# Two PSUM results of a graph-attention layer leave PSUM through ScalarE and are taken up later by VectorE

## The chip, the cores and the metric

The kernel runs on one core of a Trainium2 chip. The metric is the device time of one execution in microseconds (us), as the median of several runs. Five engines work side by side, each through its own instructions in order: TensorE (PE; its weight loads are listed apart as PEld), VectorE (DVE), ScalarE (ACT), GpSimd (POOL) and SyncE (SP, which issues most of the transfers). They wait for each other by semaphores.

## The reference

`x` has 6250 nodes of 768 features; 100000 directed edges come sorted by destination (`dst`), with random sources (`src`). To these edges each node adds a loop to itself.

```python
def gat_conv(h, W, a_src, a_dst, heads):          # one attention layer
    h = (h @ W).reshape(n, heads, -1)
    alpha_s = (h * a_src[None]).sum(-1)
    alpha_d = (h * a_dst[None]).sum(-1)
    e = leaky_relu(alpha_s[src] + alpha_d[dst], 0.2)
    e = exp(e - segment_max(e, dst)[dst])
    alpha = e / segment_sum(e, dst)[dst]
    return segment_sum(h[src] * alpha[:, :, None], dst)

h = maximum(layernorm(x), 0)
h = relu(gat_conv(h, W1, ..., heads=4) + b1)      # layer 1: 4 heads of 64
h = relu(gat_conv(h, W2, ..., heads=1) + b2)      # layer 2: 1 head of 256
out = x + relu(h @ Wm1 + bm1) @ Wm2 + bm2         # 256 -> 256 -> 768
```

## The kernel before

**Stages.** The profile's span has four of them: features of all nodes (layer norm, `h @ W1`; up to about 200 us), the edges of layer 1 (about 205 to 1350 us), a border (to about 1450), and the edges of layer 2 with the closing MLP. Nodes lie in 49 tiles of 128 (`NT`). Edges lie in tiles of 128, four tiles to a group (`TPG`), 196 groups (`NG`), four groups to a "tile step" `t` (`t, j = divmod(g, 4)`). One loop runs over the groups `g`; the order of each engine's instructions is the order in which this loop writes them out (a manual schedule), and the waits follow from who reads and writes which buffer.

**A group.** GpSimd gathers the table rows of the sources by indirect transfers, eight groups ahead (`gather(g + 8)`, L645, one transfer per edge tile). Rows of two edge tiles are a pair, and each group has two. For a pair (`pair`, L712, L722, L724) VectorE forms the weight of each edge per head from the row's own factors and the destination's factors and scales the row by it into `hw` (10 buffers). TensorE multiplies `hw` with a 0/1 matrix `hot` (5 buffers, written by VectorE at L673 for the next group), which adds up the rows by destination in `o_ps` (L736, three PSUM banks, one for two groups). Every second group VectorE adds such a product to the running sum (L753) and ScalarE copies its finished quarters (`sum`, L762). When a node tile is complete, its node step runs in pieces over the following half groups (`Node1.steps`): VectorE adds the tile's own loop (`mine` from L939, sum at L945), divides (L956, L958), TensorE turns the result (L915), ScalarE adds the bias and clips (`rT`, L921), TensorE multiplies by `W2` (L966), ScalarE writes the next table's row tile (`kept`, L969 and the lines after it), and SP stores it.

**Destination factors.** The factors of the destinations reach the edges by a product too. VectorE builds a 0/1 mask for eight edge tiles (`make_mask`, L662, from rows fetched at L610; SP also stores it for layer 2), and TensorE multiplies each edge tile's mask with the window of node factors (`meet`, L691, 16 tiny matmuls a tile step). The products come in three parts per head, which VectorE adds up in place in PSUM (`join`, L699); `pair` works in that same PSUM tile `e_ps`, of which there are two. In the loop, `meet(t + 1)` is written at j = 0 and `join(t + 1)` at the end of j = 3.

**Completing rows.** 46 edge tiles of layer 1 (23 pairs, list `SOON`) are gathered early, during the first stage, when the last m node tiles are not yet computed (m from 2 to 20). Those rows are held in DRAM, brought back in time (`soon_back`), and what they lack is added by products with the feature tiles that stayed in SBUF. For pair number i and half t (k = 2i + t) VectorE compares the sources with the m missing tiles' node numbers (`soon_hits`, L379, into `soon_hit`, 128 x up to 2560, one buffer in a pool with `bufs=1`), TensorE makes the m products (`soon_missing`, L389, into a PSUM bank of tag "n", two banks shared with the node steps), and VectorE adds them to the row (`soon_whole`, L396):

```python
row = G[soon_pair[i]][:, t]
nc.vector.scalar_tensor_tensor(row, row, soon_ok[:, i, t:t + 1], soon_p.pop(k),
                               ALU.mult, ALU.add)
```

One pair is due every eight groups. For pair i the groups are: even half, hits in 8i + 1, products in 8i + 3, taken up in 8i + 5; odd half, hits in 8i + 5, products in 8i + 6, taken up in 8i + 8. The pair itself is used in group 8i + 11. Within a group the hook stands between the two pairs, the taking up ahead of the next hits.

PSUM's eight banks in this stage: three of `o_ps`, two of tag "n", two of tag "e" (`e_ps`), one of constants.

Of the kernel before, what the change touches and what calls it, by code (L numbers as in the profile page):

```python
# [10 lines left out]
F32 = mybir.dt.float32  # L11
BF16 = mybir.dt.bfloat16
I32 = mybir.dt.int32
AF = mybir.ActivationFunctionType
ALU = mybir.AluOpType
# [55 lines left out]
def kernel(  # L71
# [99 lines left out]
        nc.sync.dma_start(wt, WT.rearrange("(j p) f -> p j f", p=P))  # L171
        return wt, a

    def scores_in(ps, w, wt, a, K, H):
        nc.vector.tensor_copy(w[:, :, HID:], scores(ps, wt, a, K, H))

    def scores(ps, wt, a, K, H):
        p = ps.tile([P, K, 2 * H], F32, name="aps", tag="e")
        for k in range(K):
            for j in range(KH):  # L180
                nc.tensor.matmul(p[:, k], wt[:, j, k * P:(k + 1) * P], a[:, j],
                                 start=(j == 0), stop=(j == KH - 1))
        return p
# [151 lines left out]
    soon_i = const.tile([P, len(SOON), 2], I32, name="soon_i")  # L335
    soon_ok = const.tile([P, len(SOON), 2], F32, name="soon_ok")
    soon_d = dram.tile([len(SOON), P, 2 * TW[1]], F32, name="soon_d")
    soon_G, soon_of, soon_p, soon_hit = {}, {}, {}, {}
    soon_pair = {i: pair for pair, i in SOON_AT.items()}

    def soon_places(i):
# [42 lines left out]
    def soon_missing(k):  # L384
        if 0 <= k < 2 * len(SOON):
            there, hit = SOON[k // 2], soon_hit.pop(k)
            soon_p[k] = ps.tile([P, TW[1]], F32, name="missing1", tag="n")
            for T in range(there, NT):
                nc.tensor.matmul(soon_p[k], hit[:, T - there], kept[T], start=(T == there),  # L389
                                 stop=(T == NT - 1))  # L390

    def soon_whole(G, k):
        if 0 <= k < 2 * len(SOON):
            i, t = divmod(k, 2)
            row = G[soon_pair[i]][:, t]
            nc.vector.scalar_tensor_tensor(row, row, soon_ok[:, i, t:t + 1], soon_p.pop(k),  # L396
                                           ALU.mult, ALU.add)

    mask_d = dram.tile([NU * P, 8 * P], BF16, name="mask_d")
# [219 lines left out]
    def layer_edges(layer, H, node, pre, matched, pre_pool):  # L619
# [4 lines left out]
        with tc.tile_pool(name=f"eg{layer}", bufs=5) as eg, \  # L624
                tc.tile_pool(name=f"hw{layer}", bufs=10 if layer == 1 else 14) as hwp, \
                tc.tile_pool(name=f"sum{layer}", bufs=4) as sums, \
                tc.tile_pool(name=f"sm{layer}", bufs=4) as sm:
            G, hot, e_ps, o_ps = {}, {}, {}, {}

            def tiles(g):  # L630

# [51 lines left out]
            def meet(t):  # L683

                if t >= NT:
                    return
                e_ps[t] = ps.tile([P, 16, 6 * H], F32, name="e_ps", tag="e")
                for u, at, a, b in ranges(t):
                    m = mask.pop(u)
                    for k in range(a, b):  # L690
                        nc.tensor.matmul(e_ps[t][:, at + k, :3 * H], m[:, k * P:(k + 1) * P],  # L691
                                         pre.win[:, 2 * u + 2], start=True, stop=True)

            def join(t):
                if t >= NT:
                    return
                (_, _, a, _), (_, at, _, b) = ranges(t)
                T = slice(a, at + b)
                nc.vector.tensor_reduce(  # L699
                    e_ps[t][:, T, 3 * H:4 * H],  # L700
                    e_ps[t][:, T, :3 * H].rearrange("p t (h k) -> p t h k", k=3), AX.X, ALU.add)

            def pair(g, p):

                if 2 * p not in tiles(g):
                    return
                Gp = G.pop(TPG // 2 * g + p)
                e1, e2 = ((Gp[:, :, RW[1]:RW[1] + 4], Gp[:, :, RW[1] + 4:]) if layer == 1 else
                          (Gp[:, :, HID:HID + 1], Gp[:, :, HID + 2:]))
                at = TPG * (g % 4) + 2 * p  # L710
                rho, v, w = (e_ps[g // 4][:, at:at + 2, k * H:(k + 1) * H] for k in range(3, 6))
                nc.vector.tensor_mul(v, e2, rho)  # L712
                if layer == 2:
                    w = sm.tile([P, 2, H], F32, name="w")
                    nc.vector.tensor_max(w, v, e1)  # L715
                    hw = hwp.tile([P, 2, P], F32, name="hw")
                    for t in range(2):
                        k = TPG * g + 2 * p + t
                        nc.vector.tensor_scalar(hw[:, t], iota_ps, dcol[:, k:k + 1], w[:, t],  # L719
                                                ALU.is_equal, ALU.mult)  # L720
                else:
                    nc.vector.tensor_max(w, v, e1)  # L722
                    hw = hwp.tile([P, 2, H, C + 1], F32, name="hw")
                    nc.vector.tensor_mul(  # L724
                        hw, Gp[:, :, :RW[1]].rearrange("p t (h c) -> p t h c", h=H),
                        w.unsqueeze(3).to_broadcast([P, 2, H, C + 1]))
                u = g // 2
                if u not in o_ps:
                    o_ps[u] = ps.tile([P, RW[layer]], F32, name="o_ps", tag="o", bufs=3)
                for t in range(2):  # L730
                    k = 2 * p + t
                    if layer == 2:
                        l, r = hw[:, t], Gp[:, t]
                    else:
                        l, r = hot[g][:, k], hw[:, t].rearrange("p h c -> p (h c)")
                    nc.tensor.matmul(o_ps[u], l, r[:, :RW[layer]], start=(g % 2 == 0 and k == 0),  # L736
                                     stop=(g % 2 == 1 and k == tiles(g)[-1]))
# [74 lines left out]
            if layer == 2:  # L812
                first_whole(pre_pool, layer)
            meet(0)
            join(0)
            def taken_up(h):

# [27 lines left out]
            for g in range(NG):  # L845
                t, j = divmod(g, 4)
                if layer == 2 and g >= NG - 2:
                    if g == NG - 2:
                        last_pairs()
                    continue  # L850
                if g == NG - 2:
                    at_end.append(g)
                gather(g + AHEAD)
                pair(g, 0)
                if g == NG - 1:
                    pair(g, 1)
                if g == NG - 2:
                    gather_up(NU - 2)
                advance(g)
                if taken_up(2 * g) is not None:  # L860
                    gather_up(taken_up(2 * g))
                if g <= NG - 4:
                    make_hot(g + 1)
                if g in (NG - 4, NG - 3):
                    make_hot(g + 2)
                if j == 0:
                    if layer == 1:
                        fetch_rows(t + 4)
                    node.prefetch(t)
                    meet(t + 1)  # L870
                elif j == (2 if t < NT - 1 else 1):
                    node.ahead(t)
                elif j % 2:
                    make_mask((g + 7) // 2)
                if layer == 1:
                    for i, at in enumerate(SOON_GROUP):
                        for k, hits_at in ((2 * i, at - 10), (2 * i + 1, at - 6)):
                            if g == hits_at + 3 + (k % 2 == 0):
                                soon_whole(G, k)
                            if g == hits_at:  # L880
                                soon_hits(pre_pool, k)
                            if g == hits_at + 1 + (k % 2 == 0):
                                soon_missing(k)
                        if g == at - 13:
                            soon_sources(pre_pool, i)
                if g == NG - 3:
                    idle_ps.append(ps.tile([P, 4 * P], F32, name="idle_ps", tag="e"))
                if g >= NG - 3:
                    stay_warm(3)
                if g < NG - 1:  # L890
                    pair(g, 1)
                advance(g, 1)
                if j == 3:
                    join(t + 1)
                if taken_up(2 * g + 1) is not None:
                    gather_up(taken_up(2 * g + 1))
                if NG - 3 <= g < NG - 1:
                    stay_warm(3)
                hot.pop(g, None)
                if layer == 1 and g == NG - 6:  # L900
                    first_sources(2)
# [23 lines left out]
    with tc.tile_pool(name="w2p", bufs=1) as wp, tc.tile_pool(name="wk2", bufs=2) as wk:  # L925
# [4 lines left out]
        class Node1:  # L930
# [4 lines left out]

            def ahead(self, t):
                C = HID // 4
                self.mine[t] = wk.tile([P, 4, C + 1], F32, name="mine")
                nc.vector.tensor_mul(self.mine[t], heads_row(kept[t]),  # L939
                                     pre1.own[:, t].unsqueeze(2).to_broadcast([P, 4, C + 1]))  # L940

# [6 lines left out]
            def steps(self, t, sum_, most=None, last=None):  # L948
                C = HID // 4
                if most is None:  # L950
                    all_ = self.whole(t, sum_)
                else:
                    all_ = wk.tile([P, 4, C + 1], F32, name="all_")
                    nc.vector.tensor_add(all_, most, last.rearrange("p (h c) -> p h c", h=4))
# [20 lines left out]
        with tc.tile_pool(name="pre1", bufs=1) as pre:  # L975
            pre1 = prepare(pre, 1, 4)
            layer_edges(1, 4, Node1(), pre1,
                        lambda: scores_in(ps, w2, *w2_in, KH, 1), pre)


    with tc.tile_pool(name="wmp", bufs=1) as wp, tc.tile_pool(name="x3", bufs=4) as xp, \
# [454 lines left out]
```

## Time and profile before

| | |
|---|---|
| time, median of 4 runs | 2580.72 us (2571.19 to 2584.02) |
| profiled execution, time | 2583.54 us |
| profiled execution, span | 2581.7 us |
| TensorE busy | 1800.1 us (70%) |
| VectorE busy | 1390.0 us (54%) |
| ScalarE busy | 411.7 us (16%) |
| GpSimd busy | 1527.8 us (59%) |
| granted TensorE clock, mean | 0.797 |

An instruction group in the profile reads: line, engine, operation, output <- inputs, shapes, count | busy us, mean ns of one | idle time of the engine just ahead of them, with what released it. The waits list who waited for whom: total us, how often, the longest. In a timeline a line has its start, its duration, engine, line, operation, and in brackets the idle time before it. "remote" as a releaser means that the profile found no releaser on this core; "issue" is time in which the engine waited for nothing that the profile shows.

### The profile page before, as it was taken

The numbers are of one execution on the slowest core, as the hardware profiler recorded it, in microseconds if no ns is written. First come the engines' busy times: TensorE is split into PE (matmuls) and PEld (weight loads), VectorE is DVE, ScalarE is ACT, GpSimd is POOL, SyncE is SP. The second block draws the span as 40 slices with busy tenths as digits, with TensorE's granted clock in tenths as the row PEclk, the third lists the DMA queues.
The fourth block names the chain that finished last, engine by engine and source line by source line (L and its number), as shares of the span: only waits on it lengthen the run. The fifth ranks groups of instructions, "written<-read, shape, count | busy, mean of one in ns | idle before, by whom it ended". The sixth has DMA issues, their size and how long they took to land.

```text
span 2581.7 us, 26527 instructions
## 1 busy us (share of the span) xinstructions
PE 1800.1 (70%) x7727; PEld 1286.7 (50%) x7729; DVE 1390.0 (54%) x4195; ACT 411.7 (16%) x1273; POOL 1527.8 (59%) x1666
## 2 busy tenths in 40 slices
PE   9853768668677667767766567677677756777677
PEld 7741546546555546545554344454344544444444
DVE  7642567567666667566665444445344444444444
ACT  6640011011111111111111011111111111111111
POOL 5347465566566556556554566666666666666661
PEclk9975788878789778788878667778777777777788
DMA  9976354455455455445543445445454545445442
GB/s 354 332 239 223 112 148 141 139 139 158 137 156 155 128 148 154 142 138 150 143 114 121 122 123 152 139 147 155 147 156 130 153 150 154 135 149 152 146 149 73
DMA packets 167327, 400.36 MB, mean 155 GB/s; under 512 B 36631, under 2 KB 54254, under 8 KB 167174
## 3 DMA queue, kind: packets, MB, share of 16 engines
q0 software_dynamic: 75072, 211.10, 29.8%
q1 hardware_dynamic: 90732, 185.99, 21.2%
q10 hardware_dynamic: 1370, 1.48, 0.2%
q8 instruction: 65, 1.06, 0.2%
q14 instruction: 88, 0.72, 0.1%
HBM read 333.87 MB, written 64.56 MB: 154 GB/s over the span
## 4 chain that ended last, share of the span: by engine, by line
PE 34%; issue 22%; DVE 20%; another core or an unknown queue 15%; POOL 4%; DMA 3%; ACT 2%; SPq 0%; DVEq 0%; ACTq 0%; POOLq 0%
PE o_ps L736 17%; PE y_ps L1088 5%; PE h_ps L447 4%; POOL G L645 4%; DVE hot L673 4%; DVE hw L724 3%; PE missing L389 3%; DMA G<-table,src_i 3%; DVE soon_hit L379 2%; DVE e_ps L722 2%; DVE e_ps L712 2%; PE tp L1078 1%; DVE acc L753 1%; DVE hw L719 1%
## 5 line engine op out<-in xcount | busy, mean ns | idle before, releaser
L645 POOL DMA_INDIRECT G<-table,src_i x1507 | 1435.4, 952 | 871.0 <-issue 380.0
L736 PE MATMUL o_ps<-G,hw 128*128 128x258 f32 x1564 | 517.5, 460 | 217.4 <-issue 179.3
L736 PE MATMUL o_ps<-hw,hot 128*128 128x260 f32 x1564 | 500.2, 459 | 204.7 <-issue 124.8
L736 PEld LDWEIGHTS o_ps<-G,hw 128*128 128x128 f32 x1564 | 349.7, 230 | 362.3 <-issue 262.0
L736 PEld LDWEIGHTS o_ps<-hw,hot 128*128 128x128 f32 x1564 | 334.8, 224 | 337.6 <-issue 168.3
L762 ACT ACTIVATE sum<-acc 32x260 f32<-32x260 f32 (+1 forms) x384 | 160.7, 418 | 1310.8 <-DVE acc L753 785.6
L389 PE MATMUL missing<-kept,soon_hit 128*128 128x268 f32 x1028 | 265.2, 410 | 61.1 <-issue 60.6
L719 DVE TENSOR_SCALAR hw<-iota_ps,dcol,w 128x128 f32<-128x128 f32 x782 | 285.0, 406 | 16.0 <-DVE w L715 1.7
L724 DVE TENSOR_TENSOR hw<-G,e_ps 128x520 f32<-128x520 f32 x391 | 271.8, 695 | 25.8 <-DVE e_ps L722 8.4
L389 PEld LDWEIGHTS missing<-kept,soon_hit 128*128 128x128 f32 x1028 | 205.5, 202 | 115.1 <-issue 77.6
L1092 DVE TENSOR_TENSOR y<-y_ps,xt 128x384 f32<-128x384 f32 (+1 forms) x98 | 54.6, 557 | 267.9 <-PE o_ps L736 102.5
L1088 PE MATMUL y_ps<-wm,mT 128*128 128x384 f32 x392 | 183.5, 598 | 19.7 <-issue 16.3
L447 PE MATMUL h_ps<-w,r 128*128 128x264 f32 (+1 forms) x588 | 140.9, 394 | 21.7 <-ACT r L437 21.1
L396 DVE SCALAR_TENSOR_TENSOR G<-G,soon_ok,missing 128x268 f32<-128x268 f32 x46 | 22.6, 492 | 240.1 <-remote 196.0
L673 DVE TENSOR_TENSOR hot<-iota_ps,dcol 128x512 f32<-128x512 f32 x196 | 133.6, 682 | 28.4 <-remote 18.7
L691 PE MATMUL e_ps<-win,mask 128*128 128x12 bf16 (+1 forms) x1564 | 72.6, 167 | 104.8 <-issue 96.5
L447 PEld LDWEIGHTS h_ps<-w,r 128*128 128x128 f32 x588 | 110.3, 194 | 44.9 <-ACT r L437 23.6
L1088 PEld LDWEIGHTS y_ps<-wm,mT 128*128 128x128 f32 x392 | 78.7, 223 | 106.5 <-issue 74.2
L712 DVE TENSOR_TENSOR e_ps<-G,e_ps 128x8 f32<-128x8 f32 (+1 forms) x782 | 126.4, 162 | 5.9 <-issue 1.6
L691 PEld LDWEIGHTS <-mask 128*128 128x128 bf16 x1564 | 63.1, 98 | 112.8 <-issue 100.8
L1083 ACT ACTIVATE mT<-tp,bm1c 128x128 f32<-128x128 f32 x98 | 30.8, 365 | 512.2 <-PE o_ps L736 223.0
L753 DVE SCALAR_TENSOR_TENSOR acc<-acc,keep,o_ps 128x260 f32<-128x260 f32 (+1 forms) x192 | 91.6, 477 | 12.4 <-issue 5.9
(415 smaller groups left out, 1278.5 us busy)
## 6 DMA issues: line engine op xcount, KB each, us to landing
xt<-in_x SPq DMA_DIRECT2D x96, 384.0 KB
drow<-dmod_d SPq DMA_DIRECT2D x49, 512.0 KB
mask_d<-mask SPq DMA_DIRECT2D x97, 256.0 KB
mask<-mask_d SPq DMA_DIRECT2D x97, 256.0 KB
G<-table,src_i POOLq DMA_INDIRECT x1507
xTt<-in_xT SPq DMA_DIRECT2D x49, 384.0 KB
out<-y SPq DMA_DIRECT2D x48, 384.0 KB
table<-kept SPq DMA_DIRECT2D x49, 134.0 KB
```

Source lines behind the costliest of these rows:

```text
L389: nc.tensor.matmul(soon_p[k], hit[:, T - there], kept[T], start=(T == there), stop=(T == NT - 1))
L447: nc.tensor.matmul(h_ps[:, :n], r[:, k], w1[:, k, :n], start=(k == 0), stop=(k == KI - 1))
L645: nc.gpsimd.indirect_dma_start(out=G[k // 2][:, k % 2], out_offset=None, in_=table[layer], in_offset=bass.IndirectOffsetOnAxis(ap=src_i[:, ...
L673: nc.vector.tensor_tensor(hot[g][:, T[0]:T[0] + n], iota_ps.unsqueeze(1).to_broadcast([P, n, P]), dcol[:, k:k + n].unsqueeze(2).to_broadca ...
L691: nc.tensor.matmul(e_ps[t][:, at + k, :3 * H], m[:, k * P:(k + 1) * P], pre.win[:, 2 * u + 2], start=True, stop=True)
L712: nc.vector.tensor_mul(v, e2, rho)
L719: nc.vector.tensor_scalar(hw[:, t], iota_ps, dcol[:, k:k + 1], w[:, t], ALU.is_equal, ALU.mult)
L724: nc.vector.tensor_mul(hw, Gp[:, :, :RW[1]].rearrange("p t (h c) -> p t h c", h=H), w.unsqueeze(3).to_broadcast([P, 2, H, C + 1]))
L736: nc.tensor.matmul(o_ps[u], l, r[:, :RW[layer]], start=(g % 2 == 0 and k == 0), stop=(g % 2 == 1 and k == tiles(g)[-1]))
L753: nc.vector.scalar_tensor_tensor(acc, run[0], keep[:, u % 2:u % 2 + 1], o_ps.pop(u), ALU.mult, ALU.add)
L762: nc.scalar.activation(done[t][r], acc[r], AF.Copy)
L1088: nc.tensor.matmul(y_ps, mT[:, j], wm2[:, j, s * half:(s + 1) * half], start=False, stop=(j == KH - 1))
```

## The change

Three things change in layer 1, and a little in layer 2 that follows from the banks.

1. ScalarE copies the product of each completing half from PSUM to SBUF (`soon_out`, three buffers) in the groups in which VectorE took it up so far. VectorE takes up both halves of a pair in group 8i + 10, from the copy.
2. The parts of the destination factors have one PSUM bank (`parts`), and the joined factors have another one (`factors`, halves for even and odd tile steps). In layer 1 `meet` runs a tile step earlier (`meet(t + 2)` at j = 0), ScalarE copies its result to SBUF at the end of j = 3 (`parts_out(t + 2)`), and `join(t + 1)` reads the copy made four groups before. Masks are built two steps of two groups earlier for it (`g + 11` for `g + 7`), with an order of its own for the first tile step. Layer 2 keeps `meet(t + 1)`, and its join reads PSUM as before.
3. A node step of layer 1 begins one group later (`rest(2)`), except at the end, and `mine` has three buffers.

The numbers of instructions on TensorE, VectorE, GpSimd and SyncE stay; ScalarE has 95 more (46 and 49 copies).

```diff
@@ the completing rows
+    def soon_out(pool, k):
+        if 0 <= k < 2 * len(SOON):
+            soon_m[k] = pool.tile([P, TW[1]], F32, name="soon_m", bufs=3)
+            nc.scalar.activation(soon_m[k], soon_p.pop(k), AF.Copy)
+
     def soon_whole(G, k):
...
-            nc.vector.scalar_tensor_tensor(row, row, soon_ok[:, i, t:t + 1], soon_p.pop(k),
+            nc.vector.scalar_tensor_tensor(row, row, soon_ok[:, i, t:t + 1], soon_m.pop(k),
                                            ALU.mult, ALU.add)
@@ the destinations' parts
+            parts = {}
+            factors = ps.tile([P, 2, 16, 3 * H], F32, name="factors", tag="factors", bufs=1)
...
-                e_ps[t] = ps.tile([P, 16, 6 * H], F32, name="e_ps", tag="e")
+                parts[t] = ps.tile([P, 16, 3 * H], F32, name="e_parts", tag="parts", bufs=1)
...
-                        nc.tensor.matmul(e_ps[t][:, at + k, :3 * H], m[:, k * P:(k + 1) * P],
+                        nc.tensor.matmul(parts[t][:, at + k], m[:, k * P:(k + 1) * P],
                                          pre.win[:, 2 * u + 2], start=True, stop=True)
+            def parts_out(t):
+
+                if t >= NT:
+                    return
+                to = sm.tile([P, 16, 3 * H], F32, name="parts_sb", bufs=3)
+                nc.scalar.activation(to[:, met(t)], parts[t][:, met(t)], AF.Copy)
+                parts[t] = to
 
             def join(t):
...
+                e_ps[t] = factors[:, t % 2]
                 nc.vector.tensor_reduce(
-                    e_ps[t][:, T, 3 * H:4 * H],
-                    e_ps[t][:, T, :3 * H].rearrange("p t (h k) -> p t h k", k=3), AX.X, ALU.add)
+                    e_ps[t][:, met(t), :H],
+                    parts.pop(t)[:, met(t)].rearrange("p t (h k) -> p t h k", k=3), AX.X, ALU.add)
@@ the loop over groups
-                    meet(t + 1)
+                    if layer == 2 or t == 0:
+                        meet(t + 1)
+                    if layer == 1 and t > 0:
+                        meet(t + 2)
                 elif j == (2 if t < NT - 1 else 1):
                     node.ahead(t)
-                elif j % 2:
-                    make_mask((g + 7) // 2)
+                elif j % 2 and (layer == 2 or t > 0):
+                    make_mask((g + (11 if layer == 1 else 7)) // 2)
+                if layer == 1 and t == 0:
+                    for u in ((), (4, 5), (6,), (7,))[j]:
+                        make_mask(u)
+                    if j == 1:
+                        parts_out(1)
+                    if j == 2:
+                        meet(2)
                 if layer == 1:
                     for i, at in enumerate(SOON_GROUP):
                         for k, hits_at in ((2 * i, at - 10), (2 * i + 1, at - 6)):
                             if g == hits_at + 3 + (k % 2 == 0):
+                                soon_out(sm, k)
+                            if g == at - 1:
                                 soon_whole(G, k)
...
                 if j == 3:
+                    if layer == 1:
+                        parts_out(t + 2)
                     join(t + 1)
@@ the node step
-                self.mine[t] = wk.tile([P, 4, C + 1], F32, name="mine")
+                self.mine[t] = wk.tile([P, 4, C + 1], F32, name="mine", bufs=3)
...
                 if most is None:
+                    if not at_end:
+                        yield from rest(2)
                     all_ = self.whole(t, sum_)
```

More of the change, by code (lines that the diff above doesn't have):

```diff
@@ L172, in weights_in, with scores_in, scores @@
         return wt, a
[L174 to L178, printed above, removed]
+    def scores_in(ps, w, wt, a, K, H, tag="e", bufs=None):
+        nc.vector.tensor_copy(w[:, :, HID:], scores(ps, wt, a, K, H, tag, bufs))
+    def scores(ps, wt, a, K, H, tag, bufs):
+        p = ps.tile([P, K, 2 * H], F32, name="aps", tag=tag, **({"bufs": bufs} if bufs else {}))
         for k in range(K):
@@ L337 @@
     soon_d = dram.tile([len(SOON), P, 2 * TW[1]], F32, name="soon_d")
-    soon_G, soon_of, soon_p, soon_hit = {}, {}, {}, {}
+    soon_G, soon_of, soon_p, soon_hit, soon_m = {}, {}, {}, {}, {}
     soon_pair = {i: pair for pair, i in SOON_AT.items()}
@@ L690, in meet, with met @@
                     for k in range(a, b):
-                        nc.tensor.matmul(e_ps[t][:, at + k, :3 * H], m[:, k * P:(k + 1) * P],
+                        nc.tensor.matmul(parts[t][:, at + k], m[:, k * P:(k + 1) * P],
                                          pre.win[:, 2 * u + 2], start=True, stop=True)
+            def met(t):
+                (_, _, a, _), (_, at, _, b) = ranges(t)
+                return slice(a, at + b)
+            def parts_out(t):
[4 more added lines that the diff above has]
+                parts[t] = to
             def join(t):
@@ L696, in join @@
                     return
-                (_, _, a, _), (_, at, _, b) = ranges(t)
-                T = slice(a, at + b)
+                e_ps[t] = factors[:, t % 2]
                 nc.vector.tensor_reduce(
-                    e_ps[t][:, T, 3 * H:4 * H],
-                    e_ps[t][:, T, :3 * H].rearrange("p t (h k) -> p t h k", k=3), AX.X, ALU.add)
+                    e_ps[t][:, met(t), :H],
+                    parts.pop(t)[:, met(t)].rearrange("p t (h k) -> p t h k", k=3), AX.X, ALU.add)
             def pair(g, p):
@@ L710, in pair @@
                 at = TPG * (g % 4) + 2 * p
-                rho, v, w = (e_ps[g // 4][:, at:at + 2, k * H:(k + 1) * H] for k in range(3, 6))
+                rho, v, w = (e_ps[g // 4][:, at:at + 2, k * H:(k + 1) * H] for k in range(3))
                 nc.vector.tensor_mul(v, e2, rho)
@@ L814, in layer_edges @@
             meet(0)
+            if layer == 1:
+                parts_out(0)
             join(0)
@@ L886, in layer_edges @@
                 if g == NG - 3:
-                    idle_ps.append(ps.tile([P, 4 * P], F32, name="idle_ps", tag="e"))
+                    idle_ps.append(ps.tile([P, 4 * P], F32, name="idle_ps", tag="parts", bufs=1))
                 if g >= NG - 3:
@@ L893, in layer_edges @@
                 if j == 3:
+                    if layer == 1:
+                        parts_out(t + 2)
                     join(t + 1)
@@ L977 @@
             layer_edges(1, 4, Node1(), pre1,
-                        lambda: scores_in(ps, w2, *w2_in, KH, 1), pre)
+                        lambda: scores_in(ps, w2, *w2_in, KH, 1, "parts", 1), pre)
     with tc.tile_pool(name="wmp", bufs=1) as wp, tc.tile_pool(name="x3", bufs=4) as xp, \
```

## The prediction, made before the change was run

> **What bounds the kernel now.** I read the windows by stage first, because only layer 1 is changed. Layer 1 in its even part is 300 to 1350 us, 177 groups of 5.94 us each.
>
> ```profile
> core 0: us, PE busy (x) PEld busy (x) DVE busy (x) ACT busy (x) POOL busy (x), PEclk, DMA share, GB/s
> 300.00:1350.00 1050.00, 758.85 (x3327) 566.72 (x3326) 670.98 (x1747) 120.14 (x434) 625.70 (x657) 0.82 0.50 143
> ```
>
> No engine is full: TensorE 72%, VectorE 64%, GpSimd 60%, ScalarE 11%. The stage is set by waits that hand over from engine to engine. The chain that ended last says the same over the whole span: VectorE's own work carries a fifth of it.
>
> ```profile
> PE 34%; issue 22%; DVE 20%; another core or an unknown queue 15%; POOL 4%; DMA 3%; ACT 2%; SPq 0%; DVEq 0%; ACTq 0%; POOLq 0%
> ```
>
> The waits of that stretch name the places (engine, line, releaser: us in all, times, longest):
>
> ```profile
> DVE G L396 <- remote: 187.3, 24, 9.5
> ...
> PE o_ps L736 <- issue: 111.1, 95, 2.9
> ...
> DVE e_ps L699 <- remote: 79.2, 11, 13.4
> ...
> PE o_ps L736 <- DVE hw L724: 46.3, 45, 1.7
> ...
> DVE G L396 <- PE missing L389: 25.9, 9, 5.8
> ...
> DVE G L396 <- PE e_ps L691: 13.6, 3, 8.8
> ```
>
> VectorE stands 227 us at L396 (taking up the completing product) and 79 us at L699 (summing the destinations' parts). On one core "remote" can only be a releaser that the trace lacks; both read a TensorE result. TensorE stands for VectorE about 66 us (46.3, and 20 more in smaller rows), and 205 us on "issue" (111.1 at L736, 73.2 at L691, 21.2 at L389). The timeline shows one such wait.
>
> ```profile
> 599.78 1.29 PE L389 MATMUL missing<-kept,soon_hit 128*128 128x268 f32 x5
> ...
> 605.11 0.95 POOL L645 DMA_INDIRECT G<-table,src_i  x1 [0.30 <-issue]
> 605.58 0.17 PE L691 MATMUL e_ps<-win,mask 128*128 128x12 bf16 x1 [1.23 <-issue]
> ...
> 608.48 0.49 DVE L396 SCALAR_TENSOR_TENSOR G<-G,soon_ok,missing 128x268 f32<-128x268 f32 x1 [8.84 <-remote]
> 608.89 2.42 DVE L379 TENSOR_TENSOR soon_hit<-soon_of,iota_ps 128x2176 f32<-128x2176 int32 x1
> ...
> 612.60 0.94 POOL L645 DMA_INDIRECT G<-table,src_i  x1 [6.53 <-DVE hw L724]
> ...
> 629.77 0.49 DVE L396 SCALAR_TENSOR_TENSOR G<-G,soon_ok,missing 128x268 f32<-128x268 f32 x1 [7.56 <-remote]
> ...
> 633.34 0.68 DVE L379 TENSOR_TENSOR soon_hit<-soon_of,iota_ps 128x512 f32<-128x512 int32 x1
> ```
>
> The product's last matmul was over at 601.07, but VectorE went on at 608.48. In between GpSimd issued gathers without a pause, and TensorE's tiny L691 matmuls crept, 1.23 us of nothing ahead of each. Both the creeping and the wait ended some 2.4 us after the last gather (606.06). The wait is about 8.8 us at first halves and 7.56 at second halves, whether the product has 12 or 20 matmuls. So most of these 227 us are not a product that takes long; they are a TensorE that answers late while gathers are issued, and the gathers pause only when VectorE's stop leaves them without buffers.
>
> **The change, step by step.** The profiled run took 2583.5 us (span 2581.7 and 1.8 around it), 2.8 above the median of 2580.7. I take savings off the median.
>
> *The hidden wait.* L396 goes to five (even) or two (odd) groups later and reads a copy; but `soon_hit` has one buffer. L379 for product k+1 therefore has to wait until product k has read it, which so far L396 ahead of it covered. For an even k, L379 stands in the same group as L396 did (8i+5): the wait stays, under another line. For an odd k, L396 stood in group 8i+8 and L379 stands in 8i+9: the wait comes one group of VectorE's work later. By the timeline that is 633.34 − 629.77 = 3.57 us. Reading the twenty odd waits of the stretch one by one, fifteen are longer than that and five shorter by 10.4 together: 20 × 3.57 − 10.4 = 61 us of VectorE work can move into waits. Even waits: nothing.
>
> *The join.* It reads a product made a tile earlier, so its 11 waits go. Next behind it is L673, writing `hot` (5 buffers), which waits for TensorE to have read the tile of five groups before, as far back as the join's product. It starts 1.68 us later (621.53 against 619.85): 11 × 1.68 = 18 us. Together 61 + 18 = 79 us of work is done in what was standing time; nobody else gains unless VectorE's work carries the chain. I take its share there, 20%: 79 × 0.20 = 16 us. The bounds: all 79, and below nothing (second rival).
>
> *Cheaper reads.* L396 takes 492 ns from PSUM; the nearest SBUF row (L939, 260 columns) takes 428: 46 × 0.065 = 3 us. L699 (360 ns, 49 times) hardly changes: 0 to 3, taken as 0.
>
> *New copies.* 46 of 128x268 and 49 of 128x192 on ScalarE. The nearest PSUM copy:
>
> ```profile
> L969 ACT ACTIVATE kept<-h_ps 128x256 f32<-128x256 f32 x43 | 15.7, 364 | 125.0 <-remote 104.6 <-PE o_ps L736 13.3 <-issue 7.1
> ```
>
> At 364 ns at most, some 35 us on an engine that is 11% busy. Queued behind a copy that waits for its product are L762 (the sums), L921 and L969; VectorE's node step needs the sums. The `rest(2)` puts a group between; the sums come a group and a half, 8.9 us, behind the copy, more than the 7.56 of an odd wait. Taken as 0; without that cover, up to 23 × 7.56 = 174 us, all of it waits that stand today on VectorE, so no loss beyond today's.
>
> The page "VectorE: DVE Perf Modes" of the Trainium skill, section "Rules for kernel authors", speaks against these copies: copy out of PSUM first only if many operations follow, else accept the slow read. Here one operation follows each copy, and the row's gain is the 65 ns above, so by the rule the 35 us of copies would buy 3 us. It weighs operations, not waits, and ScalarE has the room, so I go by the rows.
>
> *Single bank for the parts.* L691 for tile t+2 waits for the copy of t+1, issued at the end of the group before: ScalarE then has at most L969 and three tiny ones (0.36 + 3 × 0.15) and the copy (0.36) to do, 1.2 us, with a pair's 8 matmuls (some 3.5 us at 459 ns) ahead of it on TensorE. Nothing; uncovered, 49 × 1.2 = 59. Layer 2 has the wait too, but the join it waits for precedes what TensorE needs from VectorE anyway: 0.
>
> *Masks two steps earlier, `mine` with a third buffer, `rest(2)`.* Same instructions, and SP's 97 mask transfers each go a little ahead of the gathers' buffers: 0; the ends of layers lose at most half a group, 3 us; the mask builder L662 needs rows one tile (24 us) after their fetch instead of two, and shows no idle time now. At the start the join's 24 us (211 to 235 us) stays. In all 0 to +3.
>
> Sum: −16 − 3 = −19, so 2562, with −82 to +3 as this case's own ends; I hold −40 to 0 likely, 2541 to 2581, since 79 us falls into waits that are ended by the gathers, not by VectorE.
>
> **Rivals.**
>
> *Full decoupling (2515).* If VectorE runs far enough ahead that TensorE never waits for it, the 66 us go: 2581 − 66 = 2515. For it: TensorE's 72% is the largest share. Against: `soon_hit` holds the even waits where they are, and TensorE's 205 us on issue do not depend on VectorE.
>
> *Longer gather runs (2617, slower).* VectorE works 3.57 us on after each odd product, frees buffers, and GpSimd issues 3.57 / 1.255 = 2.8 gathers more (0.95 and a 0.30 gap each) before it pauses, at every second half. TensorE then creeps that much longer: 20 × 3.57 = 71, less the 19 gained = +52 at most. For it: in the blocks where L396 did not stop VectorE, creeping lasted about 20 us, and 16 groups took 94.7 to 96.3 us against 92.5 to 94.7: 1.9 more, × 11 = +21. The middle is +36: 2617. It decides once a gather run exceeds some 12 (15 us) and the next VectorE instruction waits for TensorE; runs of 8 or fewer showed no creeping. Against: the total of gathers is fixed, so a longer run is followed by a longer rest.
>
> *Nothing moves (2581).* The change then doesn't do what it says: L379 and L673 take both waits over in full, since what ends them is the last gather. 2575 to 2590.
>
> **How the numbers follow.** Forecast 0.45, longer gather runs 0.30, nothing moves 0.13, full decoupling 0.12. A measurement of this kernel tells about 0.5% from no change, 13 us: 2568 and 2594. Faster: 0.32 of the forecast, all of decoupling, 0.01 of nothing = 0.45. Same: 0.11 + 0.10 + 0.01 = 0.22. Slower: 0.29 of the runs, 0.02 each of the others = 0.33. The range goes from 2518 (decoupling's better half left out, 0.07) to 2620 (the upper third of the runs, 0.11). The forecast's own is 2541 to 2581.
>
> **What would show it.** Right: even waits near 8.8 us turn up at L379, odd ones shrink towards 4 us there, no wait at the join, some at L673; ScalarE about 35 us busier; VectorE no busier; TensorE's wait for L724 down by 10 to 20 us. Longer runs: gather runs over 12 and more than 205 us of TensorE "issue" in layer 1. Decoupling: waits at L379 mostly gone and TensorE over 76% busy. I am wrong at the root if L379 shows no wait at all, or if layer 2 changes by over 5 us.

## The result, and the profile after

The changed kernel takes 2585.56 us (median of 52 runs) against 2581.14 for the kernel before (78 runs): a ratio of 1.0018 (1.0010 to 1.0026), 4.4 us slower. The likeliest case, 2562, did not come. The time that came is that of the rival that had 0.13, nothing moves; the traces show that much moved inside. The profiled execution has a span of 2589.3 us against 2581.7.

The same stretch of layer 1 by windows (columns as in the prediction), and the chain that ended last:

```profile
300.00:1350.00 1050.00, 739.44 (x3321) 566.85 (x3320) 666.41 (x1722) 148.95 (x520) 622.73 (x648) 0.80 0.50 141
```

```profile
PE 28%; issue 24%; DVE 20%; another core or an unknown queue 15%; POOL 5%; DMA 4%; ACT 1%; SPq 1%; DVEq 0%; POOLq 0%; ACTq 0%
```

GpSimd gets 648 gathers into the 1050 us instead of 657. VectorE is idle for 1050 − 666 = 384 us, and was for 1050 − 671 = 379. So no standing time was won (ScalarE is 29 us busier with the copies). The waits of that stretch tell where VectorE stands now:

```profile
DVE soon_hit L379 <- remote: 158.4, 20, 10.5
...
PE o_ps L754 <- issue: 126.1, 99, 2.5
...
DVE hot L680 <- remote: 49.2, 9, 7.9
...
DVE factors L740 <- remote: 32.7, 13, 3.8
...
DVE soon_hit L379 <- PE missing L389: 20.7, 4, 6.8
...
PE o_ps L754 <- DVE hw L742: 10.9, 15, 1.6
```

L401 (the old L396) and L717 (the old L699) no longer wait for TensorE. L379 does, 192 us in all its rows (L396 had 229); `hot` at L680 57 us (2 before). So VectorE stands 56 us less at the places that the change touches (L396 and L699, now L379, L680 and L717). But 61 us came elsewhere: the pairs have 92 (66 before), and the node step 38 (3 before), 25 of them at its sum:

```profile
DVE all__9464 L979 <- issue: 15.8, 1, 15.8
```

TensorE's idle time in the same stretch tells the other half. It stands 29 us for VectorE (60 before), so the freed work did reach it, but 275 us on "issue" (216 before). Two waits in the timeline:

```profile
601.77 0.94 POOL L652 DMA_INDIRECT G<-table,src_i  x1 [0.30 <-issue]
...
605.10 2.42 DVE L379 TENSOR_TENSOR soon_hit<-soon_of,iota_ps 128x2176 f32<-128x2176 int32 x1 [7.90 <-remote]
...
627.84 0.95 POOL L652 DMA_INDIRECT G<-table,src_i  x1 [0.30 <-issue]
628.03 0.59 PE L754 MATMUL o_ps<-hw,hot 128*128 128x260 f32 x1 [2.34 <-issue]
...
630.83 0.17 PE L698 MATMUL e_parts<-win,mask 128*128 128x12 bf16 x1 [1.91 <-issue]
...
631.53 0.52 PE L698 MATMUL e_parts<-win,mask 128*128 128x12 bf16 x14 [0.53 <-issue]
...
631.63 0.69 DVE L379 TENSOR_TENSOR soon_hit<-soon_of,iota_ps 128x512 f32<-128x512 int32 x1 [9.92 <-remote]
```

VectorE again goes on 2.4 and 2.8 us after the last gather of a run (its end at 602.71 and 628.79), when TensorE takes up its pace again. Until then TensorE starts only at multiples of 0.70 us: from 628.03 to 630.83 are four of them, to 631.53 one more. The second wait is one of a comparison behind an odd product: it comes a group later, and it is longer (9.9 against 7.6), not shorter. Counting GpSimd's runs of gathers with less than 0.6 us between them: before, 11 of 83 have 14 gathers and more; after, 29 of 54. Where before has 23 runs of 12, after has runs of 14 and of 16. The stretches in which TensorE starts only at multiples of 0.70 us grew from 318 to 374 us; another count, of two or more such steps in a row, gives 303 and 382. Nine blocks of sixteen groups, at the same place of the pattern, took 861 us together before and 871 after. All this is one trace of each kernel.

### The profile page after: what moved, and what is told of

It is laid out like the page before. It is cut to its first block, busy times and chain, and to the rows that moved or that the text cites. A ratio compares the mean times of both kernels' runs of the same rounds, so it can differ in the third digit from the quotient of the medians.

```text
span 2589.3 us, 26650 instructions
## 1 busy us (share of the span) xinstructions
PE 1775.9 (69%) x7727; PEld 1292.8 (50%) x7729; DVE 1394.9 (54%) x4195; ACT 443.3 (17%) x1368; POOL 1533.2 (59%) x1666
## 4 chain that ended last, share of the span: by engine, by line
PE 28%; issue 24%; DVE 20%; another core or an unknown queue 15%; POOL 5%; DMA 4%; ACT 1%; SPq 1%; DVEq 0%; POOLq 0%; ACTq 0%
PE o_ps L754 15%; POOL G L652 5%; PE y_ps L1124 4%; DVE hw L742 4%; PE h_ps L452 3%; DVE hot L680 3%; DMA G<-table,src_i 3%; DVE factors L740 2%; DVE factors L730 2%; PE missing L389 2%; DVE acc L771 2%; DVE hw L737 2%; PE tp L1114 1%; DVE mask L669 1%
## 5 line engine op out<-in xcount | busy, mean ns | idle before, releaser
L754 PE MATMUL o_ps<-hw,hot 128*128 128x260 f32 x1564 | 476.3, 440 | 193.4 <-issue 151.0
L754 PEld LDWEIGHTS o_ps<-hw,hot 128*128 128x128 f32 x1564 | 327.8, 217 | 300.6 <-issue 197.3
L742 DVE TENSOR_TENSOR hw<-G,factors 128x520 f32<-128x520 f32 x391 | 271.9, 695 | 32.8 <-DVE factors L740 16.7
L389 PEld LDWEIGHTS missing<-kept,soon_hit 128*128 128x128 f32 x1028 | 205.9, 202 | 92.4 <-issue 51.6
L698 PE MATMUL e_parts<-win,mask 128*128 128x12 bf16 (+1 forms) x1564 | 75.0, 167 | 186.5 <-issue 136.9
L379 DVE TENSOR_TENSOR soon_hit<-soon_of,iota_ps 128x1408 f32<-128x1408 int32 (+18 forms) x46 | 75.5, 1641 | 197.5 <-remote 158.4
L680 DVE TENSOR_TENSOR hot<-iota_ps,dcol 128x512 f32<-128x512 f32 x196 | 133.7, 682 | 73.2 <-remote 65.2
L730 DVE TENSOR_TENSOR factors<-G,factors 128x8 f32<-128x8 f32 (+1 forms) x782 | 126.4, 162 | 10.9 <-issue 5.4
L740 DVE TENSOR_TENSOR factors<-factors,G 128x8 f32<-128x8 f32 x391 | 68.2, 175 | 63.3 <-remote 36.2
```

The lines of the kernel that those rows point to most:

```text
L680: nc.vector.tensor_tensor(hot[g][:, T[0]:T[0] + n], iota_ps.unsqueeze(1).to_broadcast([P, n, P]), dcol[:, k:k + n].unsqueeze(2).to_broadca ...
L698: nc.tensor.matmul(parts[t][:, at + k], m[:, k * P:(k + 1) * P], pre.win[:, 2 * u + 2], start=True, stop=True)
L742: nc.vector.tensor_mul(hw, Gp[:, :, :RW[1]].rearrange("p t (h c) -> p t h c", h=H), w.unsqueeze(3).to_broadcast([P, 2, H, C + 1]))
```

## The experiments

Two theories at first. **G**: the gathers pace layer 1 and make TensorE answer late, so VectorE's standing time is only where the slack shows. **B**: the one buffer of `soon_hit` holds VectorE. In r1 to r5 the kernel before took 2560.63 us. The changed kernel was not run beside them; "over the changed kernel" takes it at its 1.0018 of before.

**r1, room for two hit matrices** (the even half's products run from the last tile down, so that what overlaps is read first):

```diff
-            soon_hit[k] = pool.tile([P, NT - SOON_FROM, P], F32, name="soon_hit")
+            if "ring" not in soon_hit:
+                soon_hit["ring"] = pool.tile([P, 30, P], F32, name="soon_hit")
+            soon_hit[k] = soon_hit["ring"][:, 30 - m:] if t else soon_hit["ring"][:, :m]
...
```

> The changed kernel, with room for two hit matrices (30 tiles; even halves at one end, odd ones at the other, so that up to 15 tiles each lie apart). Theory G (gathers pace the loop: TensorE answers late while GpSimd gathers without a pause, and VectorE's standing time is only where the loop's slack shows): the 186 us that VectorE waits at L379 in layer 1 fall under 60, the waits at hot and at the pairs (57 and 54 us) grow by as much, and the time stays within 10 us of the changed kernel, 0.998 to 1.006 of before. Theory B (the one buffer of soon_hit is what holds VectorE): the wait goes and 40 to 66 us with it, 0.975 to 0.986 of before.

0.9998 of before (0.9967 to 1.0029). Its waits in the same stretch:

```profile
DVE hot L683 <- remote: 139.0, 21, 12.0
...
DVE soon_hit L381 <- remote: 15.6, 2, 7.8
...
DVE all__4357 L982 <- ACT sum L783: 13.7, 1, 13.7
```

The wait at the comparison is gone (192 to 19 us in all rows). `hot` took some 100 us of it, and the node step's sum at L982 nearly as much: it stands 122 us, most of it for the sums that ScalarE copies behind its waiting copies of the products. VectorE's idle time in all hardly falls (371 us against 384), and the 0.70 us stretches stay (391 us by the second count). B's 0.975 to 0.986 lies outside the interval: the wait moves to whichever instruction next needs something of TensorE, directly or through ScalarE. G had the time right, and the node step not in it.

**r2, every comparison made twice** (the whole `tensor_tensor` of L379 written a second time):

> The changed kernel, with every comparison of L379 made twice in a row: 46 more VectorE instructions of 1.64 us in the mean, 75 us. Theory G: the work goes into time in which VectorE would stand, +0 to +15 us over the changed kernel, 1.002 to 1.008 of before. Theory V (VectorE's own work sets the pace between its waits, as the prediction had it for a fifth): a fifth would be +15, all of it +75, 1.007 to 1.031.

1.0199 of before (1.0145 to 1.0253), some 47 us over the changed kernel for 75 us of work. G's expectation missed; the result lies in V's range. VectorE's work is not free just because VectorE stands elsewhere: this work, right behind a wait, counted by some six tenths. That is a net price. The 0.70 us stretches are shorter in this trace than in that of the changed kernel (305 against 382 us by the second count), and the second comparison also delays the product that reads it, so the work alone may cost more; no run has the same work at another place.

**r3, pauses between gathers**, in layer 1 (`nap` is a 128x128 scratch tile):

```diff
                     nc.gpsimd.indirect_dma_start(
...
+                    naps[0] += 1
+                    if layer == 1 and naps[0] % 8 == 0:
+                        for _ in range(6):
+                            nc.gpsimd.memset(nap, 0.0)
```

> The changed kernel, with six short memsets on GpSimd after every eighth gather of layer 1 (some 1.3 us, 90 times, 115 us more on GpSimd), so that no more than eight gathers follow each other without a pause. Theory G: the stretches in which TensorE starts only every 0.70 us (374 us of them in the even part of layer 1) fall below half, the longest waits of VectorE shrink under 5 us, and 20 to 60 us are saved, 0.98 to 0.995 of before. Rival P (GpSimd's total work sets the pace, 0.95 and a 0.30 gap per gather, 820 of 1050 us): +30 to +115 us, 1.013 to 1.047. Theory B: within 5 us of the changed kernel.

0.9627 of before (0.9589 to 0.9664), 98 us saved although GpSimd has 118 us of memsets more. Its waits from 300 to 1250 us (layer 1 ends earlier):

```profile
DVE factors L736 <- DMA G<-table,src_i: 218.7, 135, 4.8
...
PE o_ps L760 <- issue: 32.4, 34, 4.2
```

VectorE now waits for gathered rows; its waits at L379 are 5.3 us in all. The 0.70 us stretches went from 374 to 5 us. G had forecast 20 to 60 us, so it was short in size; P and B are out. This shows the cause of the waits: uninterrupted gathers were what made TensorE late there, and TensorE's lateness was what VectorE stood for.

**r5, every second tile's rows by a plain load** (the rows are not those of the edges' sources):

```diff
+                    if layer == 1 and k % 2:
+                        nc.sync.dma_start(G[k // 2][:, k % 2], table[layer][k % 48 * P:k % 48 * P + P])
+                        continue
```

> The changed kernel, but in layer 1 every second edge tile's rows come as one plain load of 128 table rows that SyncE issues, as many bytes, so GpSimd gathers only half as often (the rows are then not those of the edges' sources). Theory G: the 0.70 us stretches vanish, VectorE's long waits go, and 60 to 200 us are saved, 0.92 to 0.977 of before. If it is the bytes that make TensorE late, or theory B: within 20 us of the changed kernel, 0.994 to 1.01.

0.8564 (0.8514 to 0.8613), 370 us saved, more than G's 200. The trace has none of the 0.70 us stretches from 205 to 990 us, with as many bytes per tile: so it is the gathers, not the bytes. Whether it is GpSimd's issuing or the scattered rows this run doesn't separate, and part of the 370 us is simply that half as many gathers take less time on GpSimd.

**All later runs** (s, t, v and w) fell where the kernel before took 2095 to 2101 us. They can be read only with that in mind, and its reason stays open; whether it goes with the chip, as some expectations below put it, is not shown, since the record has chip 7 for r1 to r5 and for the s and v runs alike. I wanted to know whether the change pays once the runs are capped (theory **E**: longer runs ate the gain) or not at all (**N**), and what a pause must be.

> The kernel before, with the same pauses on GpSimd as r3 (six memsets after every eighth gather of layer 1). Theory E (the freed VectorE time was worth something, but longer gather runs ate it): with the runs capped at eight the change must show its worth, so this one is slower than the changed kernel with pauses by the prediction's 19 us or more: 0.970 to 0.985 of the kernel before. Rival N (the waits that the change moves are worth nothing in any case): the same as the changed kernel with pauses, 0.959 to 0.967.

> The changed kernel, with one memset in place of six after every eighth gather (0.21 us, with its gap some 0.5). If any instruction between the gathers is enough: under 40 us of 0.70 us stretches in layer 1, and GpSimd 85 us less busy than with six, 0.93 to 0.963 of before. If the length of the pause counts: over 200 us of such stretches and 0.985 to 1.003.

> The changed kernel, with three memsets after every eighth gather (0.64 us and a gap). If any instruction is enough: between one and six, 0.94 to 0.963. If the length counts: part of the stretches left, 0.96 to 0.99.

> The changed kernel, with the six memsets after every eighth gather in both layers. Layer 2 has 337 us of 0.70 us stretches in the changed kernel. Theory G: they go there too, and 20 to 100 us more are saved: 0.92 to 0.955 of before. Rival P (GpSimd's total work sets layer 2's pace): layer 2 gets longer by up to 110 us, 0.965 to 1.005.

Measured against before: before with pauses 1.0776 (1.0756 to 1.0796), one memset 1.0043 (1.0030 to 1.0056), three 1.0445 (1.0424 to 1.0465), six in both layers 1.141 (1.1389 to 1.1431). All expectations missed, since there is nothing to cure here and GpSimd's pauses lengthen the run of gathers: one, three and six memsets at 92 places cost 9, 94 and 162 us. That is not by number: one memset of 0.23 us lies mostly in the gap of 0.30 us that stands between two gathers anyway. What a pause must be where TensorE is late these runs can't tell. The plain kernels come next.

> The changed kernel as it is, beside the others of this call. The kernel before took 2560 us on the chip of the first call and 2095 on that of the second. On a chip of the first kind: 1.000 to 1.005 of before. On one of the second kind, where the kernels with pauses showed no 0.70 us stretches: theory E (longer gather runs ate the gain) has nothing to eat it there, so the prediction's 19 us or more, 0.975 to 0.992; rival N (the moved waits are worth nothing): 0.997 to 1.005.

> The kernel before with six memsets after every eighth gather of layer 1. First kind of chip, theory E: 0.970 to 0.985, slower than the changed kernel with the same pauses by 19 us or more; rival N: 0.959 to 0.967, the same. Second kind: 1.076 to 1.080 as before.

> The changed kernel with the same pauses. First kind: 0.959 to 0.967 as before. Second kind: GpSimd's total work sets the pace, so within 0.004 of the kernel before with pauses.

> The changed kernel with one memset after every eighth gather. First kind: if any instruction between the gathers is enough to keep TensorE from the 0.70 us stretches, 0.90 to 0.963; if the length of the pause counts, 0.985 to 1.003. Second kind: 1.003 to 1.006 as before.

The changed kernel: 1.0000 (0.9989 to 1.0011). Pauses: before 1.0758 (1.0742 to 1.0775), after 1.0770 (1.0753 to 1.0786); one memset 1.0032 (1.0020 to 1.0044). The changed kernel has N's time and the pauses cost both kernels the same; but where nothing makes TensorE late, that doesn't decide between E and N.

> The kernel before itself, for its profile on this call's chip. Where it takes some 2560 us: 0.70 us stretches of about 318 us and 227 us of VectorE's waiting at L396 in layer 1. Where it takes some 2100: none of these stretches, under 20 us at L396, and gathers end to end (theory G: the waits that the change moves are there only where gathers make TensorE late).

> The kernel before with six memsets after every eighth gather of layer 1. Where before takes some 2560: theory E (longer gather runs ate the gain) 0.970 to 0.985, slower than the changed kernel with pauses by 19 us or more; rival N (the moved waits are worth nothing) 0.959 to 0.967, the same. Where it takes 2100: 1.075 to 1.079.

> The changed kernel with the same pauses. Where before takes some 2560: 0.959 to 0.967. Where it takes 2100: 1.075 to 1.079.

> The changed kernel with one memset after every eighth gather. Where before takes some 2560: 0.90 to 0.963 if any instruction between the gathers is enough to spare TensorE the 0.70 us stretches, 0.985 to 1.003 if the length of the pause counts. Where it takes 2100: 1.002 to 1.005.

The kernel before, run as an experiment: 1.0000 (0.9990 to 1.0011); pauses 1.0770 (1.0750 to 1.0791) before and 1.0773 (1.0754 to 1.0793) after; one memset 1.0052 (1.0034 to 1.0070). The kernel before here, by windows (layer 1, whose last pair is at 1094 us, and the 100 us behind it) and by waits from 300 to 1000 us:

```profile
205.00:1200.00 995.00, 827.18 (x3918) 628.14 (x3918) 788.29 (x2117) 143.97 (x518) 752.56 (x789) 0.90 0.62 179
```

```profile
DVE G L396 <- PE missing L389: 6.3, 8, 1.7
```

and of the changed kernel in t1, the same two views and four gathers of its timeline:

```profile
205.00:1200.00 995.00, 816.72 (x3899) 621.22 (x3898) 793.46 (x2116) 171.78 (x608) 753.29 (x790) 0.92 0.62 179
```

```profile
DVE soon_hit L379 <- PE missing L389: 5.2, 3, 2.4
```

```profile
611.55 0.94 POOL L652 DMA_INDIRECT G<-table,src_i  x1 [0.30 <-issue]
612.79 0.95 POOL L652 DMA_INDIRECT G<-table,src_i  x1 [0.30 <-issue]
614.05 0.95 POOL L652 DMA_INDIRECT G<-table,src_i  x1 [0.30 <-DVE factors L740]
615.30 0.98 POOL L652 DMA_INDIRECT G<-table,src_i  x1 [0.30 <-issue]
```

Here GpSimd gathers end to end: 790 gathers in 995 us are 1.26 us each, a gather of 0.95 and its gap of 0.30. That is the floor of layer 1, and the waits that the change moves are 6 us. So the expectation of the kernel before held in all three parts. The gathers' own duration is the same as in the first profile (953 ns); what differs is TensorE, which no longer answers late although the gathers never pause (the second count finds no 0.70 us stretch there in either kernel). The granted clock differs too, 0.90 and 0.92 here against 0.82 and 0.80, but a lower mean doesn't bring the stretches by itself: r3 has 0.84 from 300 to 1250 us, and the kernel before with pauses (s1) 0.83 from 300 to 1000 us, and both have next to none of them. Within the first trace the clock is lower inside the stretches (0.68) than outside (0.88); which brings which is not shown.

The last two runs took that floor away, before against after:

> The kernel before with every second edge tile's rows of layer 1 as a plain load by SyncE (128 table rows, as many bytes; not the rows of the edges' sources), so that gathers set the pace neither as a floor nor by making TensorE late. Theory E: then the waits that the change moves are VectorE's or TensorE's own, and this kernel is slower than the changed one with the same loads by 10 us or more. Rival N: both within 5 us of each other. Against before: 0.85 to 0.87 where before takes some 2560, 0.84 to 0.94 where it takes 2100 (the gathers are a floor of 1.25 us each, 990 of 995 us in layer 1 there, and halved).

> The changed kernel with the same plain loads. Theory E: 10 us or more (0.004 of before) faster than the kernel before with them; rival N: within 5 us. Against before: 0.851 to 0.861 where before takes some 2560, 0.84 to 0.94 where it takes 2100.

Before with plain loads 0.9503 (0.9486 to 0.9519), after 0.9471 (0.9458 to 0.9484): medians 1995.76 and 1989.83, so the change is worth 5.9 us there, between the two expectations; the intervals just part. Against before both missed their 0.84 to 0.94. Their waits from 205 to 1100 us, the kernel before first:

```profile
DVE G L396 <- PE missing L389: 33.5, 18, 4.1
```

```profile
DVE soon_hit L379 <- PE missing L389: 15.3, 11, 3.6
```

With VectorE 88% busy (790 of 895 us), 18 us of the waits that the change moves go, its idle time in all falls from 105 to 95 us, and the time by 5.9 us. 15 us of the moved wait stay, under L379.

## Why the prediction was wrong, point by point

**What bounds the kernel.** The reading of the timeline held: VectorE's long waits end when a run of gathers ends, whatever the product's size, and r3 shows that the runs cause them. The prediction said that "79 us falls into waits that are ended by the gathers, not by VectorE", but used it for its range only, not for its sum. Its 66 us of TensorE standing for VectorE are 60 in the trace's rows.

**The hidden wait.** Right that L379 takes the wait over. Behind even products it has 95.8 us (126.5 at L396 before, over the whole run), where the prediction let nothing change. Behind odd ones 61 us were to go; they went from 113.6 to 101.7, mostly as waits of 9.9 us at every second pair with next to none between, not as shorter waits at each. (The trace has 22 odd waits in the stretch, eight of them shorter than 3.57 us, so the 61 should have been 58; that isn't what failed.) What failed is the step "61 us of VectorE work can move into waits": it took the end of a wait as fixed. VectorE did work on, but the work frees buffers, the run of gathers grows from 12 to 14 and 16, and the end moves later.

**The join.** Its 79 us of waits went from the line as forecast, and `hot` took 57 of them, about the 61 that the 18 us later start leaves. This term held at its own place.

**What the sum left out.** Together 56 us of the 79 went at these places. The sum let every other wait stay as it was, and there 61 us came: 26 at the pairs, 35 in the node step. TensorE crept 56 us longer (318 to 374). So VectorE's standing time rose by 5 us instead of falling by 79, and the 16 us priced from it did not come.

**The share of 20%.** It was never put to the test, since the standing time that it prices did not go. r2 has another price, some six tenths net, for work added right behind the wait.

**Cheaper reads.** Read from SBUF, L401 takes 492 ns, what L396 took from PSUM. The 3 us, priced from another operation's row, were not there.

**New copies, single bank, masks, `rest(2)`.** Taken as nothing. The mask builder shows no wait. The single bank does once, at the start of layer 1, where TensorE waits for the copy of the parts:

```profile
PE e_parts L698 <- ACT parts_sb L710: 41.2, 1, 41.2
```

It cost nothing lasting: the changed kernel reaches pair 16 at 273 us, the kernel before at 279. The cover that the prediction named for the sums wears thin: the node step's sum stands 25 us in the changed kernel, in three waits, and 122 us in r1 (L982), once the comparisons no longer hold VectorE back. How much of the 25 us is the copies' doing is open, as the profile names ScalarE for 6 us only.

**The rivals.** "Longer gather runs" had the mechanism, and its signs came: runs over 12, and 253 us of TensorE "issue" at its three lines instead of 205. Of its price of 71 us more creeping 56 came, and the net was +4.4 us instead of +36, inside "nothing moves" (2575 to 2590). Its second leg, 1.9 us more in a block of sixteen groups, was weak: such blocks spread from 92.4 to 100.1 us in the trace before. That the time came out even is a balance: TensorE stands 32 us less for VectorE and 59 us longer on "issue". That the one made up for the other is my reading of the two traces; no run separates them where TensorE is late. With plain loads, where the runs are gone and TensorE is not late, 5.9 us of gain are left. Full decoupling did not come: TensorE is 70% busy, and r1, without the hold of `soon_hit`, has the same time.

**Open.** Why TensorE answers late during gathers in one place and not in another, with the same kernel and the same gathers, no run tells. Whether the change is worth something with pauses where TensorE is late wasn't measured, nor whether one or three memsets are pause enough there, as the later runs all fell where it is not.

## What to carry to other kernels

Before pricing a wait that is to be removed, ask what ends it, and whether the work moved into it changes that end. If it ends with another engine's run, here the gathers, then working on through it lets that engine run on, and the wait comes back later and elsewhere; break the run, or shorten it, to see whether it is the cause. Look for the floor too: gathers times their own duration and gap told the time of layer 1 that no change on VectorE could beat.

## What the runs showed of the hardware

The same kernel took 2560 to 2581 us in some groups of runs and 2095 to 2101 in others. In the former TensorE starts only at multiples of 0.70 us once GpSimd has gathered, mostly, for 10 to 16 us without a pause, and takes up its pace mostly 2.3 to 3.9 us after the last gather; six memsets of 0.21 us after every eighth gather left 5 of 374 us of that and saved 3.7% of the time. In the latter no such stretch was found in the traces of the two plain kernels, and the same pauses cost 7.6 to 7.8%. A gather of 128 rows takes 0.95 us of GpSimd and a gap of 0.30, so a run of them goes at 1.26 us each. A version that is best in both was not found.
